# Attention of two query tiles at once, with the values' matrix applied to the result, in a fused FFN–attention–FFN kernel on one core

## The chip, the cores and the metric

The kernel runs on one core of a Trainium2 chip. The metric is the device time of one execution in microseconds, here as the median of the runs shown. Engines are named as in the profile: PE (TensorE's matmuls), PEld (its weight loads), DVE (VectorE), ACT (ScalarE), POOL (GpSimd), SP (SyncE).

## The reference, cut to what matters

The input x is 8 x 1024 x 128 in fp32. Three residual steps follow one another: half of a mixture-of-experts FFN of layernorm(x) (16 experts of 64 units, four chosen per token, and a shared expert), causal attention of layernorm(x), and the same half FFN again. The change is in the attention:

```python
q = einsum('bmd,ed->bme', x, w_q); k = einsum(..., w_k); v = einsum(..., w_v)
scores = einsum('bqd,bkd->bqk', rotate(q), rotate(k)) / sqrt(d)
attn = softmax(where(causal, scores, -inf), axis=-1)
return einsum('bqk,bkd->bqd', attn, v)
```

Here x is the layernorm's output, m = 1024 and d = 128, with one head for each of the 8 sequences.

## The kernel before, in words

A sequence has 8 tiles of 128 tokens. The FFN works on a **group** of four tiles. There are two layers of FFN, 8 sequences and 2 groups each, so 32 groups, and the main loop makes one **pass** for each. A pass first computes the shared expert (L270, then ACT's `ss` at L275 and DVE's product at L276), then eight ups, then nine downs. An up is two matmuls of 512 columns (L283, L284), a Silu on ACT (L286) and a product on DVE (L288) that writes `hidT`. POOL weighs `hidT` by the routing (L292). A down is a matmul of 512 columns (L298); the ninth is followed by a copy of the result on DVE (L306).

Everything else is put by hand into **slots** between these steps: U0 before the first up, U1 to U8 after each up, D0 to D8 after each down. A slot's functions are issued in the order in which they were entered: queries, heads, groups. The order of each engine's instructions is the order of issue. A group's routing for the next pass is spread over the slots: D7 and D8 hold `route_b` (L206), `score` (L211), `top_a` and `top_b`; U1 of the following pass holds `top_c` (ending in `comb`, L243), U3 `spread` (L252), which needs `comb`. U3 also holds `add` of the pass before (L328 on PE, L331 on DVE).

**Attention.** `Heads` belongs to one sequence: it normalizes the tiles, transposes them into `hT`, projects q and k (L367 to L375; two projections, in U3 and U4, of the pass in which the head's first query is and of the pass before) and, in `values`, the values v (L381, L385). A `Query` is one tile of 128 queries, number i from 0 to 7 of its head. It goes through scores (L400 to L407), exp (L411), two `turn`s of up to four transposes each (L427, evacuated by ACT at L431 or by DVE at L433) and `attend` (L439): i + 1 matmuls of 128 columns, then one product-and-sum on DVE (L443) and the two statistics instructions of the next layernorm (L149, L150).

Queries are handed out in order, two or three to a pass. With n = 0, 1, 2 for the first, second and third query of pass p, attend stands in D7 of pass p, U2 of pass p + 1 and U5 of pass p + 1. The queries of passes 3 to 28 are, by number i: (0 1 2) (3 4) (5 6 7) (0 1) (2 3 4) (5 6) (7 0 1) (2 3) (4 5 6) (7 0) (1 2 3) (4 5) (6 7) (0 1) (2 3 4) (5 6) (7 0 1) (2 3) (4 5) (6 7) (0 1 2) (3 4) (5 6 7) (0 1 2) (3 4 5) (6 7). Heads 0 to 7 begin in passes 3, 6, 9, 12, 16, 19, 23 and 26.

**PSUM.** Ups use banks 0 to 3 by turns, so an up needs the bank that DVE's L288 of the up two before has read. The shared expert uses bank 5, projections 4 and 5, scores two banks (2 and 3, or 4 and 5). All smaller work takes banks 6 and 7 in strict turn: `other_bank()` returns the other one at each call. Whoever takes a bank waits for the engine that evacuates what was put there two calls before.

```python
def other_bank():
    spare[0] += 1
    return bank(6 + spare[0] % 2)
```

Of the kernel before, what the change touches and what calls it, by code (L numbers as in the profile page):

```python
# [9 lines left out]
F32 = mybir.dt.float32  # L10
AF = mybir.ActivationFunctionType
ALU = mybir.AluOpType
# [3 lines left out]
P = 128  # L16
# [10 lines left out]
def kernel(  # L27
# [14 lines left out]
    nc = tc.nc  # L42

    B, S, D = x.shape
    E = gate_w.shape[1]
    I = w_sh_down.shape[0]
    NT = S // P
    GT = 4
    NG = NT // GT
    W = GT * P  # L50
# [7 lines left out]
    ln = ctx.enter_context(tc.tile_pool(name="ln", bufs=2))  # L58
    small = ctx.enter_context(tc.tile_pool(name="small", bufs=3))
    work = ctx.enter_context(tc.tile_pool(name="work", bufs=3))  # L60
    big = ctx.enter_context(tc.tile_pool(name="big", bufs=2))
    att = ctx.enter_context(tc.tile_pool(name="att", bufs=2))
# [5 lines left out]
    def bank(i, n=1):  # L68
        return psum[:, i * W : (i + n) * W]
# [3 lines left out]
# [4 lines that stand above are left out]
    def tiles_of(ap):  # L77
        return ap.rearrange("p (j q) -> p j q", q=P)
# [16 lines left out]
    xs, mvs = [None] * B, {}  # L95
# [38 lines left out]
    wqkv = const.tile([P, 3, D], F32, name="wqkv")  # L134
# [8 lines left out]
    def stats(key, b, tiles):  # L143

        if key not in mvs:
            mvs[key] = small.tile([P, NT, 2], F32, tag="mv", name=f"mv_{key}", bufs=16)
        for t in tiles:
            st = small.tile([P, 6], F32, tag="st", name=f"st_{key}_{t}")
            nc.vector.bn_stats(st, xs[b][:, t, :])  # L149
            nc.vector.bn_aggr(mvs[key][:, t, :], st)  # L150

    def deviation(key, g):
        tiles = slice(g * GT, (g + 1) * GT)
        rstd = small.tile([P, GT], F32, tag="rstd", name=f"rs_{key}_{g}")
        nc.vector.tensor_scalar(rstd, mvs[key][:, tiles, 1], LN_EPS, None, ALU.add)
        nc.gpsimd.tensor_tensor(rstd, rstd, neg_half, ALU.pow)  # L156
        return rstd

    def normed(key, b, g, rstd):
        xn = ln.tile([P, GT, D], F32, tag=f"xn{key[0]}", name=f"xn_{key}_{g}")  # L160
        for j in range(GT):
            t = g * GT + j
            nc.vector.tensor_scalar(  # L163
                xn[:, j, :], xs[b][:, t, :], mvs[key][:, t, 0:1], rstd[:, j : j + 1],
                ALU.subtract, ALU.mult,
            )
        return xn

    def transposed(key, g, xn, hT):
        pt = other_bank()  # L170
        for j in range(GT):
            nc.tensor.transpose(tiles_of(pt)[:, j, :], xn[:, j, :], ident)  # L172
        nc.scalar.copy(hT, pt)
# [3 lines left out]
    class Group:  # L177
# [8 lines left out]
        def norm_b(self):  # L186
            self.xn = normed(self.key, self.b, self.g, self.rstd)

        def turn(self):
            self.hT = ln.tile([P, W], F32, tag="hT", name=f"hT_{self.nm}")  # L190
            transposed(self.key, self.g, self.xn, self.hT)
# [147 lines left out]
    class Heads:  # L339
# [5 lines left out]
        def deviations(self):  # L345
            self.rstd = [deviation(self.key, g) for g in range(NG)]
            b = self.b
            self.q = att.tile([P, S], F32, tag="q", name=f"q_{b}")
            self.k = att.tile([P, S], F32, tag="k", name=f"k_{b}")
            self.v = att.tile([P, NT, D], F32, tag="v", name=f"v_{b}")  # L350
            self.rl = small.tile([P, NT], F32, tag="rl", name=f"rl_{b}")
            self.hT = ln.tile([P, S], F32, tag="hTa", name=f"hT_{self.key}", bufs=1)
            self.xn = [None] * NG

        def norm(self, g):
            self.xn[g] = normed(self.key, self.b, g, self.rstd[g])

        def turn(self, g):
            transposed(self.key, g, self.xn[g], self.hT[:, g * W : (g + 1) * W])

        def project(self, w, g):

# [10 lines left out]
            nc.vector.tensor_tensor(r[:, cols], p, cs[:, 0, cols], ALU.mult)  # L373
            nc.gpsimd.tensor_tensor(other, other, cs[:, 1, cols], ALU.mult)
            nc.gpsimd.tensor_tensor(r[:, cols], r[:, cols], other, ALU.add)  # L375

        def values(self, g):
            pv = tiles_of(other_bank())
            for j in range(GT):
                t = g * GT + j  # L380
                nc.tensor.matmul(  # L381
                    pv[:, j, :], self.hT[:, t * P : (t + 1) * P], wqkv[:, 2, :],
                    start=True, stop=True,
                )
            nc.scalar.copy(self.v[:, g * GT : (g + 1) * GT, :], pv)  # L385

    class Query:

# [25 lines left out]
            )  # L414

        def turn(self, half):
            if half == 0:
                self.prT = att.tile([P, NT, P], F32, tag="prT", name=f"prT_{self.nm}")
                rl = self.h.rl[:, self.i : self.i + 1]
                nc.vector.reciprocal(rl, rl)  # L420
            k = half * GT
            n = min(GT, self.i + 1 - k)
            if n <= 0:
                return
            tp = tiles_of(other_bank())
            for j in range(n):
                nc.tensor.transpose(  # L427
                    tp[:, j, :], self.pr[:, (k + j) * P : (k + j + 1) * P], ident
                )
            if half == 0:  # L430
                nc.scalar.copy(self.prT[:, k : k + n, :], tp[:, :n, :])  # L431
            else:
                nc.vector.tensor_copy(self.prT[:, k : k + n, :], tp[:, :n, :])  # L433

        def attend(self):
            i = self.i
            o = other_bank()[:, :D]
            for j in range(i + 1):
                nc.tensor.matmul(  # L439
                    o, self.prT[:, j, :], self.h.v[:, j, :], start=(j == 0), stop=(j == i)  # L440
                )
            xt = xs[self.b][:, i, :]
            nc.vector.scalar_tensor_tensor(  # L443
                xt, o, self.h.rl[:, i : i + 1], xt, ALU.mult, ALU.add
            )
            stats(f"f1_{self.b}", self.b, [i])

# [13 lines left out]
    def at(p, slot, *fs):  # L463
        jobs.setdefault((p, slot), []).extend(fs)
# [3 lines left out]
    def when(p, slot):  # L468
        return p * len(slots) + slots.index(slot)
# [5 lines left out]
    starts, done = {}, {}  # L475
    for p in range(3, 29):
        for n in range(2 if p in (15, 21) or (p % 2 == 0 and p != 26) else 3):
            if not queue:
                continue
            b, i = queue.pop(0)  # L480
            starts.setdefault(b, p)
            q = Query(heads[b], i)
            s, first, e, t0, t1, a = (
                ((p, "U7"), 4, (p, "D0"), (p, "D3"), (p, "D5"), (p, "D7")),
                ((p, "D2"), 2, (p, "D5"), (p, "D8"), (p + 1, "U0"), (p + 1, "U2")),
                ((p, "D4"), 4, (p, "D7"), (p + 1, "U3"), (p + 1, "U4"), (p + 1, "U5")),
            )[n]
            at(*s, lambda q=q, first=first: q.scores(first))
            at(*e, q.exp)
            at(*t0, lambda q=q: q.turn(0))  # L490
            at(*t1, lambda q=q: q.turn(1))
            at(*a, q.attend)
            done[b, i] = when(*a)
    assert not queue


# [1 line left out]
    for b in range(B):  # L498
        h, st = heads[b], starts[b]
        ready = when(turn_of[0, b, 1] + 1, "U7")  # L500
        if b == 0:
            p0, p1 = st - 1, st - 1
            places = ("U8", "D0", "D2", "D3", "D5", "D6", "D7", "D8")
        else:
            p0, p1 = st - 2, st - 1
            places = ("D0", "D3", "D5", "D8", "U1", "U3", "U4", "U6")
        assert ready < when(p0, places[0])
        at(p0, places[0], h.deviations)
        at(p0, places[1], lambda h=h: h.norm(0))
        at(p0, places[2], lambda h=h: h.norm(1))  # L510
        at(p0, places[3], lambda h=h: h.turn(0))
        at(p1, places[4], lambda h=h: h.turn(1))
        at(p1, places[5], lambda h=h: h.project(0, 0))
        at(p1, places[6], lambda h=h: h.project(1, 0))
        at(p1, places[7], lambda h=h: h.values(0))
        at(st, "U3", lambda h=h: h.project(0, 1))
        at(st, "U4", lambda h=h: h.project(1, 1))
        at(st, "U6", lambda h=h: h.values(1))


    for p, gr in enumerate(groups):
# [4 lines left out]
        if p == 1:  # L526
            steps = steps[1:]
            places = [(0, s) for s in ("U3", "U5", "U6", "U8", "D0", "D1", "D2", "D3", "D6")]
        elif p == 2:
            places = [(0, s) for s in ("D0", "D3", "D5", "D6", "D7", "D8", "D8", "D8")]  # L530
            places += [(p - 1, "U1"), (p - 1, "U3")]
        else:
            places = [(p - 2, s) for s in ("U5", "D1", "D4", "D5", "D7", "D7", "D8", "D8")]
# [9 lines left out]
        if gr.layer == 0:  # L543
            t = gr.g * GT
# [5 lines left out]
    for b in range(2, B):  # L550
        p = turn_of[0, b, 0]
# [126 lines left out]
```

## Time and profile before

| what | value |
|---|---|
| median of 3 runs | 1007.22 us (1007.2 to 1007.79) |
| profiled execution | 1008.41 us, span 1006.6 us |
| PE busy | 988.0 us (98%), granted clock 0.998 |
| DVE, ACT, POOL busy | 663.9, 427.4, 451.8 us |
| L439, attend's matmuls | 576 records of 128 columns |
| L381, values' matmuls | 128 records of 128 columns |
| L385, copies of v on ACT | 16, 586 ns each |
| L443 on DVE | 64, 346 ns each |

A matmul of two fp32 operands makes two records, a transpose one. A matmul's record starts when its columns begin to be issued, and its end is modelled; the distance between starts is what it takes of PE. A line of a timeline gives start, duration, engine, source line, operation, tiles written and read, and in brackets how long the engine had been idle and what ended that. A line of waits gives the engine and who waited, for whom, the total in microseconds, how often and the longest.

### The profile page before, as it was taken

The page shows a single profiled execution, that of the slowest core. Times are in us where ns is not written, and L with a number is a line of the kernel's source. Part 1 is how long each engine was busy: PE and PEld are TensorE (multiplying, and loading weights), DVE is VectorE, ACT ScalarE, POOL GpSimd, SP SyncE. Part 2 cuts the span into 40 slices and gives each one's busy share as a digit, 9 for nine tenths or more (in the row PEclk, how much of TensorE's full clock was granted, in tenths as well). Part 3 has the DMA queues.
Part 4 walks back from the last instruction along what each step waited for, and adds up shares of the span by engine and source line. Part 5 has one row for each costly group of instructions (what it writes and reads, how often), then busy time and mean ns, then how long its engine had stood idle before and what let it go on. Part 6 is the DMA issues. An engine that isn't in the chain of part 4 may idle for free.

```text
span 1006.6 us, 11516 instructions
## 1 busy us (share of the span) xinstructions
PE 988.0 (98%) x3590; PEld 516.4 (51%) x3590; DVE 663.9 (66%) x2034; ACT 427.4 (42%) x767; POOL 451.8 (45%) x382
## 2 busy tenths in 40 slices
PE   8999999999999999999999999999999999999998
PEld 5444445554555555545554555545554555455443
DVE  5766877668766667666767656776667757665542
ACT  3334435443544444443544444444444444343321
POOL 2445556244633464234634455234653355322434
PEclk9999999999999999999999999999999999999999
DMA  5645343044303532145403452134422243224440
GB/s 164 167 106 105 86 85 84 3 105 85 85 13 83 117 85 51 35 95 117 86 15 76 90 117 68 29 74 96 95 53 59 60 95 87 47 59 95 96 96 21
DMA packets 56830, 80.23 MB, mean 80 GB/s; under 512 B 3584, under 2 KB 23360, under 8 KB 56640
## 3 DMA queue, kind: packets, MB, share of 16 engines
q1 hardware_dynamic: 55488, 78.23, 34.7%
q10 hardware_dynamic: 1280, 1.26, 0.4%
q8 instruction: 28, 0.46, 0.2%
q14 instruction: 34, 0.28, 0.1%
HBM read 74.24 MB, written 5.24 MB: 79 GB/s over the span
## 4 chain that ended last, share of the span: by engine, by line
PE 89%; DVE 7%; issue 2%; ACT 1%; POOL 0%; ACTq 0%; POOLq 0%; DVEq 0%
PE psum L298 24%; PE psum L283 19%; PE psum L284 19%; PE psum L400 6%; PE psum L439 6%; PE psum L427 3%; PE psum L367 3%; PE psum L270 2%; PE psum L172 2%; DVE hidT L288 2%; PE psum L381 1%; DVE sel L237 1%; PE psum L197 1%; PE psum L328 1%; PE psum L139 1%
## 5 line engine op out<-in xcount | busy, mean ns | idle before, releaser
L292 POOL TENSOR_TENSOR hidT<-hidT,cb 128x512 f32<-128x512 f32 x256 | 323.8, 1271 | 515.7 <-DVE hidT L288 484.1
L284 PE MATMUL psum<-hT,wu 128*128 128x512 f32 x512 | 261.5, 592 | 0.6 <-DVE hidT L288 0.6
L283 PE MATMUL psum<-hT,wg 128*128 128x512 f32 x512 | 261.8, 593 | 0.0
L286 ACT ACTIVATE sg<-psum 128x512 f32<-128x512 f32 x256 | 152.7, 597 | 229.4 <-PE psum L283 216.5
L298 PE MATMUL psum<-hidT,wd 128*128 128x512 f32 x512 | 247.5, 601 | 0.0
L288 DVE TENSOR_TENSOR hidT<-psum,sg 128x512 f32<-128x512 f32 x256 | 175.4, 686 | 96.8 <-PE psum L284 93.8
L284 PEld LDWEIGHTS psum<-hT,wu 128*128 128x128 f32 x512 | 97.2, 190 | 123.4 <-issue 103.0
L298 PEld LDWEIGHTS psum<-hidT,wd 128*128 128x128 f32 x512 | 90.1, 191 | 80.9 <-issue 74.1
L283 PEld LDWEIGHTS psum<-hT,wg 128*128 128x128 f32 x512 | 88.5, 191 | 64.2 <-issue 61.6
L439 PEld LDWEIGHTS psum<-v,prT 128*128 128x128 f32 x576 | 74.4, 192 | 30.6 <-issue 26.3
L431 ACT COPY prT<-psum 128x512 f32<-128x512 f32 (+2 forms) x64 | 32.4, 506 | 108.1 <-PE psum L427 107.4
L439 PE MATMUL psum<-v,prT 128*128 128x128 f32 x576 | 74.6, 275 | 0.0
L400 PE MATMUL psum<-k,q 128*128 128x512 f32 (+2 forms) x192 | 72.4, 486 | 0.0
L443 DVE SCALAR_TENSOR_TENSOR x<-psum,rl,x 128x128 f32<-128x128 f32 x64 | 22.1, 346 | 68.3 <-PE psum L439 38.9
L163 DVE TENSOR_SCALAR xn_f<-x,mv_f,rs_f 128x128 f32<-128x128 f32 x128 | 64.9, 567 | 1.2 <-POOL rs_f L156 1.2
L427 PEld LDWEIGHTS psum<-ident,pr 128*128 128x128 f32 x288 | 36.7, 141 | 50.2 <-issue 34.2
L400 PEld LDWEIGHTS psum<-k,q 128*128 128x128 f32 x192 | 36.5, 190 | 45.9 <-issue 45.2
L406 DVE TENSOR_REDUCE top<-psum 128x1 f32<-128x128 f32 (+3 forms) x64 | 48.5, 758 | 2.2
L427 PE MATMUL psum<-ident,pr 128*128 128x128 f32 x288 | 47.4, 274 | 1.9 <-DVE x L331 1.9
L411 ACT ACTIVATE pr<-psum,top 128x128 f32<-128x128 f32 (+3 forms) x64 | 47.7, 746 | 0.3
L404 DVE TENSOR_TENSOR psum<-psum,causal 128x128 f32<-128x128 f32 x64 | 19.0, 296 | 42.4 <-PE psum L400 42.0
L275 ACT ACT_TABLE_LOAD x31 | 39.8, 1283 | 8.9 <-PE psum L270 8.8
(88 smaller groups left out, 1001.2 us busy)
## 6 DMA issues: line engine op xcount, KB each, us to landing
cb<-cd SPq DMA_DIRECT2D x124, 512.0 KB, 8.3
x<-in_x SPq DMA_DIRECT2D x16, 256.0 KB, 10.3
out_x<-x SPq DMA_DIRECT2D x15, 256.0 KB, 2.4
cb<-cd SPq DMA_DIRECT2D x8, 256.0 KB, 5.2
cd<-cT SPq DMA_DIRECT2D x32, 32.0 KB, 1.8
cs<-in_rope SPq DMA_DIRECT2D x1, 1024.0 KB, 9.8
wg<-in_w_gate ACTq DMA_DIRECT2D x2, 256.0 KB, 6.6
wu<-in_w_up ACTq DMA_DIRECT2D x2, 256.0 KB, 6.0
```

The lines of the kernel that those rows point to most:

```text
L163: nc.vector.tensor_scalar(xn[:, j, :], xs[b][:, t, :], mvs[key][:, t, 0:1], rstd[:, j : j + 1], ALU.subtract, ALU.mult,)
L283: nc.tensor.matmul(g_ps, wg[:, units], self.hT, start=True, stop=True)
L284: nc.tensor.matmul(u_ps, wu[:, units], self.hT, start=True, stop=True)
L286: nc.scalar.activation(sg, g_ps, AF.Silu)
L288: nc.vector.tensor_tensor(hid, u_ps, sg, ALU.mult)
L292: nc.gpsimd.tensor_tensor(hid, hid, self.cb[:, k, :], ALU.mult)
L298: nc.tensor.matmul(self.y, w, h, start=(k == 0), stop=(k == NP))
L400: nc.tensor.matmul(s[:, c:e], h.q[:, i * P : width], h.k[:, c:e], start=True, stop=True)
L406: nc.vector.tensor_reduce(top, s[:, :width], AX.X, ALU.max)
L411: nc.scalar.activation(self.pr[:, : self.width], self.s[:, : self.width], AF.Exp, bias=self.top, scale=SCALE, accum_out=self.h.rl[:, self. ...
L427: nc.tensor.transpose(tp[:, j, :], self.pr[:, (k + j) * P : (k + j + 1) * P], ident)
L439: nc.tensor.matmul(o, self.prT[:, j, :], self.h.v[:, j, :], start=(j == 0), stop=(j == i))
```

## The change

Instead of multiplying probabilities by v, the kernel multiplies them by the layernorm's output and applies the values' matrix to the product: (P xn) Wv instead of P (xn Wv). The projection of v and its copies go, and the head keeps `xn` for its whole life. Queries are taken in pairs, an even one and the odd one behind it. Their transposed probabilities lie side by side, `attend` is called for the odd one alone, with passes of 256 columns (128 for the last key tile, which the even query does not see), and computes the transposed product. ACT copies it to `o`. A new `values` of the query multiplies it by the values' matrix, two matmuls of 128 columns, and does both products-and-sums and both tiles' statistics. `values` stands in U0, U4 or U6 of the pass after, by the place n of the odd query; `attend` stands where that query's attend stood.

```diff
         def turn(self, half):
+            h, q = self.h, self.i % 2
             if half == 0:
-                self.prT = att.tile([P, NT, P], F32, tag="prT", name=f"prT_{self.nm}")
+                if self.i % 2 == 0:
+                    h.prT = att.tile([P, NT, 2, P], F32, tag="prT", name=f"prT_{self.nm}")
+                self.prT = h.prT
...
-                nc.scalar.copy(self.prT[:, k : k + n, :], tp[:, :n, :])
+                nc.scalar.copy(self.prT[:, k : k + n, q, :], tp[:, :n, :])
...
         def attend(self):
+
             i = self.i
-            o = other_bank()[:, :D]
-            for j in range(i + 1):
+            o = other_bank()[:, : 2 * P]
+
+            for j in [0, i] + list(range(1, i)):
+                first = 0 if j < i else P
                 nc.tensor.matmul(
-                    o, self.prT[:, j, :], self.h.v[:, j, :], start=(j == 0), stop=(j == i)
-                )
-            xt = xs[self.b][:, i, :]
-            nc.vector.scalar_tensor_tensor(
-                xt, o, self.h.rl[:, i : i + 1], xt, ALU.mult, ALU.add
-            )
-            stats(f"f1_{self.b}", self.b, [i])
+                    o[:, first:], self.h.xn[:, j, :],
+                    self.prT[:, j, first // P :, :].rearrange("p q t -> p (q t)"),
+                    start=(j == 0), stop=(j == max(i - 1, 1)),
+                )
+            self.o = work.tile([P, 2 * P], F32, tag="o", name=f"o_{self.nm}", bufs=2)
+            nc.scalar.copy(self.o, o)
+
+        def values(self):
+            op = tiles_of(other_bank())
+            for q in range(2):
+                nc.tensor.matmul(
+                    op[:, q, :], self.o[:, q * P : (q + 1) * P], wqkv[:, 2, :],
+                    start=True, stop=True,
+                )
+            for q in range(2):
+                t = self.i - 1 + q
+                xt = xs[self.b][:, t, :]
+                nc.vector.scalar_tensor_tensor(
+                    xt, op[:, q, :], self.h.rl[:, t : t + 1], xt, ALU.mult, ALU.add
+                )
+            stats(f"f1_{self.b}", self.b, [self.i - 1, self.i])
...
-            s, first, e, t0, t1, a = (
-                ((p, "U7"), 4, (p, "D0"), (p, "D3"), (p, "D5"), (p, "D7")),
-                ((p, "D2"), 2, (p, "D5"), (p, "D8"), (p + 1, "U0"), (p + 1, "U2")),
-                ((p, "D4"), 4, (p, "D7"), (p + 1, "U3"), (p + 1, "U4"), (p + 1, "U5")),
+            s, first, e, t0, t1, a, v = (
+                ((p, "U7"), 4, (p, "D0"), (p, "D3"), (p, "D5"), (p, "D7"), (p + 1, "U0")),
+                ((p, "D2"), 2, (p, "D5"), (p, "D8"), (p + 1, "U0"), (p + 1, "U2"), (p + 1, "U4")),
+                ((p, "D4"), 4, (p, "D7"), (p + 1, "U3"), (p + 1, "U4"), (p + 1, "U5"), (p + 1, "U6")),
             )[n]
...
-            at(*a, q.attend)
-            done[b, i] = when(*a)
+            if i % 2:
+                at(*a, q.attend)
+                at(*v, q.values)
+                done[b, i - 1] = done[b, i] = when(*v)
```

The head's `values`, which stood in D8 of pass 2 and U6 of pass 3 for the first head and in U6 of two neighbouring passes for the others, is gone from the lists of places, and `normed` writes into `xn` of the head, a buffer like that of v before.

More of the change, by code (lines that the diff above doesn't have):

```diff
@@ L157, in deviation, with normed @@
         return rstd
-    def normed(key, b, g, rstd):
-        xn = ln.tile([P, GT, D], F32, tag=f"xn{key[0]}", name=f"xn_{key}_{g}")
+    def normed(key, b, g, rstd, xn=None):
+        if xn is None:
+            xn = ln.tile([P, GT, D], F32, tag="xn", name=f"xn_{key}_{g}")
         for j in range(GT):
@@ L349, in deviations @@
             self.k = att.tile([P, S], F32, tag="k", name=f"k_{b}")
-            self.v = att.tile([P, NT, D], F32, tag="v", name=f"v_{b}")
+            self.xn = att.tile([P, NT, D], F32, tag="xna", name=f"xn_{self.key}")
             self.rl = small.tile([P, NT], F32, tag="rl", name=f"rl_{b}")
             self.hT = ln.tile([P, S], F32, tag="hTa", name=f"hT_{self.key}", bufs=1)
-            self.xn = [None] * NG
         def norm(self, g):
-            self.xn[g] = normed(self.key, self.b, g, self.rstd[g])
+            normed(self.key, self.b, g, self.rstd[g], self.xn[:, g * GT : (g + 1) * GT, :])
         def turn(self, g):
-            transposed(self.key, g, self.xn[g], self.hT[:, g * W : (g + 1) * W])
+            transposed(
+                self.key, g, self.xn[:, g * GT : (g + 1) * GT, :], self.hT[:, g * W : (g + 1) * W]
+            )
         def project(self, w, g):
@@ L375, in project @@
             nc.gpsimd.tensor_tensor(r[:, cols], r[:, cols], other, ALU.add)
[L377 to L383, printed above, removed]
-                )
-            nc.scalar.copy(self.v[:, g * GT : (g + 1) * GT, :], pv)
     class Query:
@@ L430, in turn @@
             if half == 0:
-                nc.scalar.copy(self.prT[:, k : k + n, :], tp[:, :n, :])
+                nc.scalar.copy(self.prT[:, k : k + n, q, :], tp[:, :n, :])
             else:
-                nc.vector.tensor_copy(self.prT[:, k : k + n, :], tp[:, :n, :])
+                nc.vector.tensor_copy(self.prT[:, k : k + n, q, :], tp[:, :n, :])
         def attend(self):
             i = self.i
-            o = other_bank()[:, :D]
-            for j in range(i + 1):
+            o = other_bank()[:, : 2 * P]
+            for j in [0, i] + list(range(1, i)):
+                first = 0 if j < i else P
                 nc.tensor.matmul(
-                    o, self.prT[:, j, :], self.h.v[:, j, :], start=(j == 0), stop=(j == i)
-                )
-            xt = xs[self.b][:, i, :]
-            nc.vector.scalar_tensor_tensor(
-                xt, o, self.h.rl[:, i : i + 1], xt, ALU.mult, ALU.add
-            )
-            stats(f"f1_{self.b}", self.b, [i])
+                    o[:, first:], self.h.xn[:, j, :],
+                    self.prT[:, j, first // P :, :].rearrange("p q t -> p (q t)"),
+                    start=(j == 0), stop=(j == max(i - 1, 1)),
+                )
+            self.o = work.tile([P, 2 * P], F32, tag="o", name=f"o_{self.nm}", bufs=2)
[14 more added lines that the diff above has]
+            stats(f"f1_{self.b}", self.b, [self.i - 1, self.i])
     LAG = 4
@@ L502 @@
             p0, p1 = st - 1, st - 1
-            places = ("U8", "D0", "D2", "D3", "D5", "D6", "D7", "D8")
+            places = ("U8", "D0", "D2", "D3", "D5", "D6", "D7")
         else:
             p0, p1 = st - 2, st - 1
-            places = ("D0", "D3", "D5", "D8", "U1", "U3", "U4", "U6")
+            places = ("D0", "D3", "D5", "D8", "U1", "U3", "U4")
         assert ready < when(p0, places[0])
@@ L514 @@
         at(p1, places[6], lambda h=h: h.project(1, 0))
-        at(p1, places[7], lambda h=h: h.values(0))
         at(st, "U3", lambda h=h: h.project(0, 1))
         at(st, "U4", lambda h=h: h.project(1, 1))
-        at(st, "U6", lambda h=h: h.values(1))
     for p, gr in enumerate(groups):
```

## The prediction

> **What bounds the kernel now.** I read the page first, then the waits of PE alone, the chain of waits, and the timeline at the seams between two passes.
>
> ```profile
> PE 988.0 (98%) x3590; PEld 516.4 (51%) x3590; DVE 663.9 (66%) x2034; ACT 427.4 (42%) x767; POOL 451.8 (45%) x382
> ...
> PE 89%; DVE 7%; issue 2%; ACT 1%; POOL 0%; ACTq 0%; POOLq 0%; DVEq 0%
> ```
>
> PE sets the end; the clock row is at 9 throughout. Two things can move the time: what PE has to issue, and where PE waits.
>
> ```profile
> PE psum L328 <- DVE x L443: 3.9, 6, 1.0
> PE psum L252 <- DVE comb L243: 2.7, 3, 2.3
> PE psum L427 <- DVE x L331: 1.9, 5, 0.4
> PE psum L252 <- DVE x L443: 1.7, 3, 0.8
> ...
> PE psum L284 <- DVE hidT L288: 0.6, 1, 0.6
> ```
>
> Those are PE's waits in the body, nearly all on DVE, and the timeline puts them in U2 to U4, just after a seam. They are counted from a modelled end; from start to start each is 0.16 longer (0.77 shown at seam 13 is 0.93). I call a seam by the pass that begins there, and count from the start of its first L270.
>
> Seam 13, after pass 12 with queries 7 and 0, from the timeline:
>
> ```profile
> 419.02 1.02 PE L270 MATMUL psum<-hT,ws 128*128 128x512 f32 x2
> ...
> 422.15 0.69 DVE L276 TENSOR_TENSOR shared<-psum,ss 64x512 f32<-64x512 f32 x1
> ...
> 422.88 0.69 DVE L288 TENSOR_TENSOR hidT<-psum,sg 128x512 f32<-128x512 f32 x1
> ...
> 424.40 1.02 PE L284 MATMUL psum<-hT,wu 128*128 128x512 f32 x2
> ...
> 425.49 0.27 DVE L243 SCALAR_TENSOR_TENSOR comb<-sel,tot 128x64 f32<-128x64 f32 x1
> ...
> 426.24 0.34 DVE L443 SCALAR_TENSOR_TENSOR x<-psum,rl,x 128x128 f32<-128x128 f32 x1
> ...
> 426.63 0.30 PE L252 MATMUL psum<-ident,comb 128*64 128x128 f32 x1 [0.77 <-DVE x L443]
> ```
>
> DVE works without a gap from L276 on. The first hidT is done at 4.55, and the third up's L284, which needs that bank, comes at 5.38: 0.8 to spare. comb is done at 6.74. PE waits at L252 for the bank that L443 frees.
>
> Seam 11, after queries 2 and 3:
>
> ```profile
> 357.56 0.60 PE L328 MATMUL psum<-ident,yT 128*128 128x128 f32 x4
> ...
> 358.96 1.02 PE L284 MATMUL psum<-hT,wu 128*128 128x512 f32 x2
> 359.02 0.69 DVE L373 TENSOR_TENSOR q<-psum,cs 128x512 f32<-128x512 f32 x1 [1.08 <-ACT o_q L372]
> ...
> 359.63 0.68 DVE L331 SCALAR_TENSOR_TENSOR x<-psum,x 128x512 f32<-128x512 f32 x1
> ```
>
> Where a projection stands in U3, L373 waits on ACT with L331 queued behind it, so the add's bank is free at 360.31, while U3's PE work ends at 359.82. Nothing asks for that bank now at this seam; five others with a turn in U4 pay 0.54 each (L427 <- L331).
>
> **Columns on PE.** The chain gives the pace of both widths:
>
> ```profile
> 416.32 1.78 PE psum L439 x16
> ...
> 433.80 0.43 PE psum L400 x2
> ```
>
> A 128-wide record is 0.1113; a 256-wide one 0.2158 (mean start to start of the 32 at L400). Per head the change issues sixteen 256-wide and four 128-wide matmuls for 36 of 128: the same columns. 128 times (4 x 0.1113 - 2 x 0.2158) = 1.7 us gained, all on the path. The values' matmuls are 64 x 2 records before and after, 14.3 us, only moved.
>
> The Trainium skill (TensorE: Matmul & The Clock Gate, Back-to-back issue gap) puts sustained matmuls at about 81 ns for 128 columns and 131 for 512, far from proportional. An estimate along that line (98 ns for 256, a record taken as one matmul) is 16 us saved, 991 in all; the rows here say otherwise.
>
> **ACT and copies.** Sixteen v copies of 0.586 go, 32 o copies of 128x256 come; the prT copy of that shape takes 0.372 (bounds 0.266 and 0.586, its 128 and 512 forms). ACT is 42% busy and between attend and values PE has at least one up (1.72) or, at U0, a down and L270 (0.86 each): nothing, and 0.2 to 0.5 a pair if that cover failed. prT is written with gaps of 128; no row shows that, the contiguous rows are nearest: nothing, at most 0.1 a copy, off the path. The weights o and xn are loaded like v (0.19, hidden).
> One consequence: the o copy at D7 stands before a third query's exp on ACT, and L270 needs bank 5, which that exp reads if the query is over 3. Copy plus 0.91 or 1.12 of exp end after L270's turn: 0.36 at seams 6 and 26, 0.15 at 28 (in their totals below).
>
> **DVE: the pair's burst.** Two L443 (0.346) and two stats now stand together, 1.55 (two steps of 0.37 and two of 0.40 between starts; one L443 with its stats takes 0.90 to the end). Where a pass's first query is odd (seams 5, 6, 9, 10, 13, 14, 19, 20, 25, 26, 28), the burst lands in U0, between L276 and the first hidT, and everything after moves with it: hidT, then comb, then L331. The even query beside it no longer attends in U2, which takes up to 1.56 of PE work out of the cover, while values add 0.445.
> Seam 13: hidT is free at 4.54 - 0.10 (no L443 in D7) + 1.55 + 0.05 = 6.04; PE arrives at 5.38 - 0.22 + 0.445 = 5.60: stall 0.44. PE would then be at L252 at 6.89 + 0.44 = 7.33; comb frees it at 6.64 + 1.60 = 8.24: 0.91 more. 1.35 against 0.93 now: +0.42.
> The 0.05 is the release that seam 3 shows (hidT ends at 5.90, L284 starts at 5.95).
> The others alike, from their own rows (hidT and comb ends now, L284's and L252's starts now, less the even query's matmuls, plus values): Seams 5 and 25: hidT 6.36 against PE 6.15, 0.21; L252 0.06 behind comb; no wait now: +0.27 each. Seams 9 and 19: 6.63 against 5.94, 0.69, and 0.06: +0.75 each. Seams 10 and 20: 6.04 against 5.60, 0.44; comb at 8.24 against 7.62, 0.62; they lose 1.16 now: -0.1 each. Seam 14: 0.44, and 8.24 against 7.82, 0.42; now 0.38: +0.48. Seams 6 and 26: hidT 0.22 later still, as ACT's ss comes behind the exp: 6.61 against 5.94, 0.67, and 0.36 at L270: +1.0 each; the 0.54 of L427 stays. Seam 28: 6.36 against 5.71, 0.65; comb 0.46; L270 0.15; a turn in U4 behind L331 0.2; now 0.40: +1.06.
>
> With seam 13 the sum is **+5.8**. Its bounds are -4.0, if all is covered and today's waits go, and 11 times the whole burst less 4.0 that they wait now, 13.
>
> The Trainium skill (PSUM — Partial Sum Buffer, Engine vs sequencer instructions) takes VectorE's queue as strict first in, first out, which speaks against this change: hidT cannot pass the burst. The rows above agree (L331 sits behind a waiting L373); were it untrue, the 5.8 would go.
>
> **Even-first seams.** The burst moves to U4, where DVE has caught up. The L443 of U2 is gone and ACT frees that bank. Of the waits now, 7 and 17 lose 0.61 each, 21 0.16. 4, 24 and 27 lose 0.72, but the spread then waits for ACT's prT copy (seam 28 shows 0.40 for 512 columns, so 0.30 for 384): 0.42 each. Sum **-2.6**. What is late next: values in U4 takes the bank of the add in U3, so where a projection stands there it meets the 0.54 of seam 11. At 8, 12 and 18 this replaces the wait of L427; at 11, 15, 16, 22 and 23 it is new: **+2.7**.
>
> **Moved work.** values(0) of head 0 stood in D8 before seam 3, where PE already waits 0.80 for hidT and DVE is bound by the projection in D7. Without its 0.89 the same wait is 0.89 longer: **+0.9**. The other heads' values leave U6, where no wait follows. Query matmuls in D7 grow or vanish, and no wait stands there: L206's input is ready 1.4 before it even without them. POOL has 3.5 or more to spare before each down.
>
> **Sum.** -1.7 + 5.8 - 2.6 + 2.7 + 0.9 = +5.1. The profiled span of 1006.6 becomes 1011.7; that execution took 1008.4 (1.8 around the span), the median is 1007.2, so 1012.3.
>
> **Rivals.**
> A, faster: DVE has more slack at the seams than one trace shows, and the burst is covered. Then the odd-first seams lose their present waits too (1.16, 0.93, 0.38, 1.16, 0.40, together 4.0): -1.7 - 2.6 - 4.0 + 3.6 = -4.7, 1002.5. It decides if hidT may come 1.55 later; the rows give 0.8.
> B, no change: the burst costs half because the stats overlap and the bank of U4 is free in time: -1.7 + 2.9 - 2.6 + 0.9 = -0.5, 1006.7. For it: single stats overlap by 0.1. Against: L331's lag is tied to PE's projection.
> C, slower still: values wait for the o copy because ACT is behind an exp, 0.2 to 0.5 for 11 to 32 pairs, some +5: 1017.3. Against it: ACT idles before most of its rows.
> That the change would not do what it says shows in no row: equal columns leave it little to do on PE.
>
> **How the numbers follow.** Forecast 0.62, A 0.12, B 0.14, C 0.12. About 0.2% (2 us) is what a measurement can tell from no change. Slower 0.62 + 0.12 = 0.74, same 0.14, faster 0.12. The range leaves out A and the far half of C, and has half a microsecond around B and C for the copies: 1006.0 to 1016.5.
>
> **What would show it.** Right: PE waits at L284 on hidT at some ten seams, at the values' line on L331 at eight, none of L328 on L443; PE's busy time down by little; the seam 13 wait at L252 on comb. Wrong: no hidT wait in U2, or values waiting on the o copy.

## The result, and the profile after

The changed kernel takes 1012.6 us (median of 6 runs, 1011.65 to 1013.52) against 1007.39 us (6 runs): 1.0052 times, 95% interval 1.0042 to 1.0062. It is slower by 5.2 us; the prediction said 1012.3. The profiled execution took 1013.49 us with a span of 1011.7.

The page of the kernel after, its busy times and its chain by engine:

```profile
PE 989.9 (98%) x3334; PEld 505.9 (50%) x3334; DVE 660.0 (65%) x2034; ACT 429.0 (42%) x783; POOL 450.1 (44%) x382
...
PE 87%; DVE 9%; ACT 2%; issue 1%; POOL 0%; ACTq 0%; DVEq 0%; POOLq 0%
```

PE has 256 records fewer and is busy for 1.9 us more, 989.9 against 988.0; DVE's share of the chain rises from 7 to 9%. No engine has much more work to do (ACT, with 16 instructions more, 1.6 us). The waits of PE alone show what it is instead. Lines have moved: up's matmuls are L284 and L285, the product that writes `hidT` L289, add L329 and L332, `comb` L244, spread L253, a turn L423, attend L438, the copy of `o` L444, values L449 and their sums L456.

```profile
PE psum L253 <- DVE comb L244: 4.4, 6, 2.3
PE psum L449 <- DVE x L332: 3.0, 8, 0.4
PE psum L173 <- DVE x L456: 2.2, 2, 1.1
PE psum L285 <- DVE hidT L289: 1.9, 5, 0.9
...
PE psum L423 <- DVE x L332: 0.8, 2, 0.4
```

The six waits of L328 on L443 and the three of L252 on it are gone. In their place stand eight of values on the add's L332, hidT and comb more often, and two of a head's turn (L173) on the sums of values, which the prediction did not have. The longest wait of the first row, 2.3, is one in pass 0 that the kernel before has too; the prediction's row of `comb` contains it, and it is no wait of the body, but its sum does not use it.

Seam 13 in the timeline of the kernel after:

```profile
419.28 1.02 PE L271 MATMUL psum<-hT,ws 128*128 128x512 f32 x2
...
422.40 0.69 DVE L277 TENSOR_TENSOR shared<-psum,ss 64x512 f32<-64x512 f32 x1
423.13 0.61 DVE L456 SCALAR_TENSOR_TENSOR x<-psum,rl,x 128x128 f32<-128x128 f32 x2
...
424.47 0.67 DVE L289 TENSOR_TENSOR hidT<-psum,sg 128x512 f32<-128x512 f32 x1
...
425.20 1.12 PE L285 MATMUL psum<-hT,wu 128*128 128x512 f32 x2 [0.15 <-DVE hidT L289]
...
427.07 0.27 DVE L244 SCALAR_TENSOR_TENSOR comb<-sel,tot 128x64 f32<-128x64 f32 x1
...
427.40 0.30 PE L253 MATMUL psum<-ident,comb 128*64 128x128 f32 x1 [0.64 <-DVE comb L244]
```

Two sums and two tiles' statistics occupy DVE from 423.13 to 424.47, between `shared` and the first hidT. The third up waits for hidT (0.32 from start to start), and L253 for comb (0.80): 1.12 where it was 0.93. In front of it PE has 0.22 of query work less and 0.445 of values more.

And values in U4 at seam 11:

```profile
358.20 0.60 PE L329 MATMUL psum<-ident,yT 128*128 128x128 f32 x4
...
359.66 0.69 DVE L376 TENSOR_TENSOR q<-psum,cs 128x512 f32<-128x512 f32 x1 [1.36 <-ACT o_q L375]
...
360.26 0.68 DVE L332 SCALAR_TENSOR_TENSOR x<-psum,x 128x512 f32<-128x512 f32 x1
...
361.00 0.71 PE L449 MATMUL psum<-wqkv,o 128*128 128x128 f32 x4 [0.38 <-DVE x L332]
```

The bank that nothing asked for before is now asked for too early, and PE loses 0.54 from start to start.

### The profile page after: what moved, and what is told of

Read it like the earlier page. It is cut to its first block, busy times and chain, and to the rows that moved or that the text cites. A ratio compares the mean times of both kernels' runs of the same rounds, so it can differ in the third digit from the quotient of the medians.

```text
span 1011.7 us, 11037 instructions
## 1 busy us (share of the span) xinstructions
PE 989.9 (98%) x3334; PEld 505.9 (50%) x3334; DVE 660.0 (65%) x2034; ACT 429.0 (42%) x783; POOL 450.1 (44%) x382
## 4 chain that ended last, share of the span: by engine, by line
PE 87%; DVE 9%; ACT 2%; issue 1%; POOL 0%; ACTq 0%; DVEq 0%; POOLq 0%
PE psum L299 24%; PE psum L285 18%; PE psum L284 18%; PE psum L438 6%; PE psum L393 6%; PE psum L423 3%; PE psum L370 2%; PE psum L271 2%; PE psum L173 2%; PE psum L449 1%; DVE hidT L289 1%; PE psum L198 1%; DVE sel L238 1%; DVE shared L277 1%; PE psum L139 1%
## 5 line engine op out<-in xcount | busy, mean ns | idle before, releaser
L285 PE MATMUL psum<-hT,wu 128*128 128x512 f32 x512 | 262.3, 594 | 2.5 <-DVE hidT L289 1.9
L284 PE MATMUL psum<-hT,wg 128*128 128x512 f32 x512 | 261.7, 593 | 0.0
L299 PE MATMUL psum<-hidT,wd 128*128 128x512 f32 x512 | 247.7, 601 | 0.0
L289 DVE TENSOR_TENSOR hidT<-psum,sg 128x512 f32<-128x512 f32 x256 | 174.3, 687 | 99.9 <-PE psum L285 95.6
L285 PEld LDWEIGHTS psum<-hT,wu 128*128 128x128 f32 x512 | 96.6, 190 | 127.7 <-issue 98.0
L299 PEld LDWEIGHTS psum<-hidT,wd 128*128 128x128 f32 x512 | 90.2, 191 | 80.9 <-issue 74.4
L284 PEld LDWEIGHTS psum<-hT,wg 128*128 128x128 f32 x512 | 90.7, 191 | 71.2 <-issue 68.2
L307 DVE COPY yT<-psum 128x512 f32<-128x512 f32 x31 | 21.4, 691 | 108.4 <-PE psum L299 108.4
L164 DVE TENSOR_SCALAR xn_f<-x,mv_f,rs_f 128x128 f32<-128x128 f32 x128 | 68.9, 598 | 1.9 <-POOL rs_f L156 1.9
L438 PE MATMUL psum<-prT,xn_a 128*128 128x256 f32 (+1 forms) x320 | 67.6, 358 | 0.0
L438 PEld LDWEIGHTS psum<-prT,xn_a 128*128 128x128 f32 x320 | 57.0, 190 | 20.7 <-issue 12.4
L423 PEld LDWEIGHTS psum<-ident,pr 128*128 128x128 f32 x288 | 36.7, 141 | 43.8 <-issue 36.9
L423 PE MATMUL psum<-ident,pr 128*128 128x128 f32 x288 | 47.2, 273 | 0.8 <-DVE x L332 0.8
L444 ACT COPY o<-psum 128x256 f32<-128x256 f32 x32 | 11.9, 372 | 83.9 <-PE psum L438 83.9
```

Of the source, the lines that this page charges most:

```text
L164: nc.vector.tensor_scalar(xn[:, j, :], xs[b][:, t, :], mvs[key][:, t, 0:1], rstd[:, j : j + 1], ALU.subtract, ALU.mult,)
L284: nc.tensor.matmul(g_ps, wg[:, units], self.hT, start=True, stop=True)
L285: nc.tensor.matmul(u_ps, wu[:, units], self.hT, start=True, stop=True)
L289: nc.vector.tensor_tensor(hid, u_ps, sg, ALU.mult)
L299: nc.tensor.matmul(self.y, w, h, start=(k == 0), stop=(k == NP))
L423: nc.tensor.transpose(tp[:, j, :], self.pr[:, (k + j) * P : (k + j + 1) * P], ident)
```

## The experiments

The theory is the prediction's: the new product costs PE nothing, and the time lies in where its follow-up work stands. The rival is that the two-step product itself (attend, copy, values) costs, wherever it stands. Where a timing is compared with a trace, I take the stretch from the first L271 (L270) of pass 2 to the end, called the body. Each body is that of one profiled execution. The first two passes, with the loads, take 63.0 to 65.1 us in these traces whichever the kernel; why they vary was not tried.

Ratios are against runs of the kernel before on the same chip, with medians of 1006.98 to 1007.39.

| kernel | median us | ratio to before, 95% | body us |
|---|---|---|---|
| before | 1006.98 to 1007.39 | | 941.7 |
| after | 1012.6 | 1.0052 (1.0042 to 1.0062) | 946.7 |
| e1, values later (first) | 1005.57 | 0.9987 (0.9978 to 0.9996) | 939.9 |
| e2, values later (second) | 1009.16 | 1.0023 (1.0014 to 1.0033) | 943.6 |
| e3, both | 1002.47 | 0.9955 (0.9941 to 0.9969) | 936.8 |
| e4, 128 columns | 1013.96 | 1.0073 (1.0060 to 1.0085) | 948.7 |
| e5, statistics apart | 1008.24 | 1.0013 (1.0004 to 1.0023) | 942.7 |
| e6, e3 and exp earlier | 1001.10 | 0.9946 (0.9933 to 0.9959) | 935.7 |
| e7, e3 and projection earlier | 1001.35 | 0.9949 (0.9936 to 0.9962) | 935.8 |
| e8, all | 1000.16 | 0.9937 (0.9923 to 0.9951) | 934.6 |
| e9, before, projection earlier | 1006.61 | 0.9992 (0.9983 to 1.0001) | 940.8 |
| e10, after, turn later | 1009.40 | 1.0018 (1.0009 to 1.0027) | 944.1 |

**e1: the burst out of U0.**

```diff
-                ((p, "U7"), 4, (p, "D0"), (p, "D3"), (p, "D5"), (p, "D7"), (p + 1, "U0")),
+                ((p, "U7"), 4, (p, "D0"), (p, "D3"), (p, "D5"), (p, "D7"), (p + 1, "U5" if p < 27 else "U4")),
```

> Values of a pair whose odd query is the first of its pass stand in U5 instead of U0 (U4 for the last such pass). Theory (DVE's burst in U0 delays hidT and comb, and the bank of values is held): the waits at the eleven odd-first seams, 9.6 us in the trace of the changed kernel, shrink to about 3.3 (comb at 13, ACT's prT copy at 10, 14, 20 and 28, the exp and L331 at 6 and 26), and the 0.1 behind each wait goes with them: 7.5 less than the changed kernel, about 1005. Rival (the time lies in the two-step product itself, attend, copy, values, wherever it stands): within 1 us of 1012.6.

Measured 1005.57; the body is 6.8 shorter than that of the changed kernel. The waits at the eleven seams fall from 9.6 to 3.5. The rival is refuted: with the same instructions, some of them in another slot, the time is 7.0 us below the changed kernel and just under the kernel before. Waits of PE in e1:

```profile
PE psum L449 <- DVE x L332: 3.0, 8, 0.4
PE psum L253 <- DVE comb L244: 2.9, 4, 2.3
...
PE psum L285 <- DVE hidT L289: 0.9, 1, 0.9
```

hidT holds PE once (at seam 3), and L173 no longer waits for L456. The eight waits of values on L332 are as they were: they belong to the other move.

**e2: values out of U4.**

```diff
-                ((p, "D2"), 2, (p, "D5"), (p, "D8"), (p + 1, "U0"), (p + 1, "U2"), (p + 1, "U4")),
+                ((p, "D2"), 2, (p, "D5"), (p, "D8"), (p + 1, "U0"), (p + 1, "U2"), (p + 1, "U5" if p < 28 else "U4")),
```

> Values of a pair whose odd query is the second of its pass stand in U5 instead of U4 (U4 for the last pass). Theory (values in U4 takes the bank of the add and waits 0.54 for L331 behind the projection): the wait goes at seams 11, 15, 16, 22 and 23 and comes back as a wait of the turn L423 at 8, 12 and 18, so 2.7 and five times 0.1 less: about 1009.4. Rival (two-step product itself): no change, 1012.6. Second rival (a full DVE queue in U4, not the bank): the wait moves to U5 with the burst, no change either, but waits stand at the ups behind U5.

Measured 1009.16, body 3.1 shorter. The waits of PE in e2 show that five are gone and three have gone back to the turn:

```profile
PE psum L423 <- DVE x L332: 1.9, 5, 0.4
```

There is no row of L449 on L332 left. The five are three new ones (seams 8, 12, 18) and the two that the changed kernel had (6, 26). It is the bank: the burst follows to U5, and no up behind it waits.

**e3: both.**

> Both moves at once. Theory: they touch different seams and add, 7.5 + 3.2 less, about 1002, below the kernel before (1007.4). Rival (two-step product itself): 1012.6. If the bursts only collide elsewhere, between 1005 and 1009.

Measured 1002.47: 0.9955 of the kernel before. The body is 9.9 shorter than the changed kernel's, the sum of 6.8 and 3.1.

Seam 13 in the timeline of e3:

```profile
417.73 0.70 DVE L277 TENSOR_TENSOR shared<-psum,ss 64x512 f32<-64x512 f32 x1
...
418.45 0.69 DVE L289 TENSOR_TENSOR hidT<-psum,sg 128x512 f32<-128x512 f32 x1
...
421.40 0.30 PE L253 MATMUL psum<-ident,comb 128*64 128x128 f32 x1 [0.19 <-DVE comb L244]
```

hidT follows `shared` at once, and 0.36 from start to start is left of 1.12.

**e4: the columns by themselves.**

```diff
-            for j in [0, i] + list(range(1, i)):
-                first = 0 if j < i else P
+            for q in range(2):
+                for j in range(i + q):
...
-                    o[:, first:], self.h.xn[:, j, :],
+                    o[:, q * P : (q + 1) * P], self.h.xn[:, j, :], self.prT[:, j, q, :],
```

> The changed kernel with attend in passes of 128 columns, one query's key tiles after the other's, so 288 matmuls again instead of 160. Theory (a record costs its columns and 3 to 4 ns more): 1.7 us more than the changed kernel, 1014.3. Rival (narrow passes are held by their weight loads, as the page's 81 ns against 131 would have it): 10 us more or over.

Measured 1013.96, body 2.0 longer. The longest attend in the chain of waits, of the kernel after and then of e4:

```profile
415.12 3.25 PE psum L438 x16
```

```profile
415.85 3.35 PE psum L438 x30
```

The same 3,840 columns, in 16 records of 0.203 (fourteen wide, two narrow) or in 30 of 0.112. From start to start all of L438 takes 62.4 us in the kernel after and 64.2 in e4. The 256-wide passes are worth 1.8 us here and no more; over 256 records that is 7 ns a record, not the 3 to 4 of the expectation. The medians differ by 1.4, and the intervals of the two ratios touch, so the size rests on the rows. An estimate from the sustained figures of the Trainium skill (TensorE: Matmul & The Clock Gate, Back-to-back issue gap), 81 ns for 128 columns and 131 for 512, gives the narrow form some 16 us more. For these fp32 matmuls the rows decide against it.

**e5: the length of the burst.** The statistics of a pair whose values stand in U0 go to U5; the sums stay.

```diff
-            stats(f"f1_{self.b}", self.b, [self.i - 1, self.i])
+        def statistics(self):
+            stats(f"f1_{self.b}", self.b, [self.i - 1, self.i])
...
+                w = (p + 1, "U5" if p < 27 else "U4") if n == 0 else v
+                at(*w, q.statistics)
```

> The changed kernel, but where values stand in U0 only the two products-and-sums stay there; the pair's statistics go to U5 (U4 for the last such pass). This takes 0.80 of the burst's 1.34 out of DVE's queue before hidT and comb, and leaves the values' matmuls, their bank and when it comes free as they were. Theory (the burst's length in DVE's queue): hidT's waits at 9, 10, 13, 14, 19, 20 go, comb's at 10, 13 and 20 halve, the bank waits stay (1.28 at seams 5 and 25, 0.87 at 6 and 26): 3.7 less than the changed kernel, 1008.9. Rival (it is the bank that values hold, or the copy of o, and not the length): 1012.6, with the same waits.

Measured 1008.24, body 4.0 shorter. Seam 13 in the timeline of e5:

```profile
420.82 0.61 DVE L456 SCALAR_TENSOR_TENSOR x<-psum,rl,x 128x128 f32<-128x128 f32 x2
...
421.35 0.68 DVE L289 TENSOR_TENSOR hidT<-psum,sg 128x512 f32<-128x512 f32 x1
...
424.28 0.30 PE L253 MATMUL psum<-ident,comb 128*64 128x128 f32 x1 [0.25 <-DVE comb L244]
```

With L271 at 416.97 the seam waits 0.41 instead of 1.12, while L456 and its bank stand where they stood. The bank waits stay to the digit: 1.28 at seams 5 and 25. So the burst costs in two separate ways at the eleven seams, by its length in DVE's queue and, at two of them, by the bank of values. The Trainium skill (PSUM — Partial Sum Buffer, Engine vs sequencer instructions) says that VectorE's queue is strict first in, first out. This agrees: with 0.8 us taken out ahead of it, hidT starts 4.38 after L271 instead of 5.19.

**e10: the bank at seams 5 and 25.**

```diff
-            places = ("D0", "D3", "D5", "D8", "U1", "U3", "U4")
+            places = ("D0", "D3", "D5", "D8", "U2", "U3", "U4")
```

> The changed kernel with the heads' second turn in U2 instead of U1 (heads 1 to 7). Theory (at seams 5 and 25 the turn waits 1.28 for the bank that the values of U0 hold until DVE reaches their two sums): a turn one up later finds the bank free and hidT ready, 2.6 less and 0.2 behind the waits, 1009.8. Rival (DVE is that late anyhow, and any PE work in its place waits): the wait goes to L285 on hidT, 1012.0 or more.

Measured 1009.40, body 2.6 shorter. One up later the turn starts without a wait, and the up behind it too, as the timeline of e10 at seam 5 shows:

```profile
157.21 0.60 PE L173 MATMUL psum<-ident,xn_a 128*128 128x128 f32 x4
157.65 1.02 PE L284 MATMUL psum<-hT,wg 128*128 128x512 f32 x2
158.51 1.02 PE L285 MATMUL psum<-hT,wu 128*128 128x512 f32 x2
```

**e6, e7, e8: what e3 leaves.** e6 moves the third query's exp ahead of the copy of `o` (`(p, "D4"), 4, (p, "D6")`), e7 head 0's projections a slot earlier (`"D7", "D5", "D6"` as the last three places), e8 both.

> Both moves of values, and the third query's exp in D6 instead of D7, ahead of the o copy on ACT. Theory (L271 waits for bank 5 because the exp is queued behind the copy of o): the 0.33 at seams 6 and 26 and the 0.11 at 28 go with 0.1 each behind them, 1.0 less than with both moves alone, 1001.5. Rival (the exp itself is late, not its place): no change, 1002.5.

> Both moves of values, and head 0's two projections of its first half one slot earlier (D5, D6), its second turn in D7. Theory (at seam 3 DVE is bound by the last projection, and the values that stood between it and the seam are gone): the waits of 1.58 at seam 3 fall to some 0.3 to 0.5, 1.3 less, 1001.2. Rival (seam 3 waits for the routing's comb and scores, whatever the projection): no change, 1002.5.

> Both moves of values, the earlier exp and the earlier projections of head 0. If each takes away a wait of its own they add: 1000.2, 0.7 per cent under the kernel before. If seam 3 only hands its wait on, 1001.5.

Measured 1001.10, 1001.35 and 1000.16. The bodies are 1.1, 1.0 and 2.2 shorter than e3's, so each takes away a wait of its own. In e6 L271 starts on time at all three seams. In e7 the waits at seam 3 are 0.54 instead of 1.58. e8 is the best version: 0.9937 of the kernel before. The page of e8:

```profile
PE 984.9 (99%) x3334; PEld 506.4 (51%) x3334; DVE 657.5 (66%) x2034; ACT 429.0 (43%) x783; POOL 450.4 (45%) x382
```

**e9: what of that is the places' own.** The kernel before with the same earlier projections.

> The kernel before the change, with head 0's two projections of its first half in D5 and D6 and its second turn in D7 (values stay in D8). How much of the gain of the best version is the places' alone: the wait of 0.80 at seam 3 and 0.1 behind it go, 0.9 less than before, 1006.2. If it were 5 us or more, the best version would owe little to the change.

Measured 1006.61, ratio 0.9992, interval up to 1.0001; the body is 0.9 shorter and seam 3 has no wait. So of the 6.8 us by which the median of e8 beats the kernel before, about one comes from this move alone. The exp's move has nothing to mend there, since no copy of `o` stands before it.

One rival was not tried: the kernel before with its other work in better slots. At seams 4 to 28 it has 10.3 us of waits from start to start, and 7.0 of them are nine waits for L443, the sum behind attend; e8 has 5.2 left. So the runs show that e8 beats the kernel as it was. They do not show how much of that the two-step product itself is worth, beyond the 1.8 of its wider passes.

## Why the prediction was right, point by point

The total is right to 0.3 us, and that closeness is luck; the terms are not all so good. Waits are counted from start to start at their seams.

**Columns**, -1.7: measured 64.2 to 62.4, -1.8, and e4 gives it back. Right.

**Odd-first seams**, +5.8: their waits went from 5.1 to 9.6, +4.5. The mechanism is shown by e1 and e5; several sizes were off, in both directions. The burst lasts 1.34, not 1.55: two sums one behind the other take 0.53 where 0.74 was taken (0.37 had been read between a sum and the statistics of its own tile), and the statistics 0.40 a tile, as taken. The 0.10 taken off for the missing L443 of D7 did not come: at seam 13 `shared` starts 3.12 after L271, and 3.13 before. And PE never waits for hidT at seams 6, 26 and 28, where 0.65 or 0.67 was expected. The timeline of the kernel after, seam 6:

```profile
188.85 1.13 PE L271 MATMUL psum<-hT,ws 128*128 128x512 f32 x2 [0.17 <-ACT pr L404]
...
191.32 0.69 DVE L277 TENSOR_TENSOR shared<-psum,ss 64x512 f32<-64x512 f32 x1
...
193.83 0.68 DVE L289 TENSOR_TENSOR hidT<-psum,sg 128x512 f32<-128x512 f32 x1
...
194.88 1.02 PE L285 MATMUL psum<-hT,wu 128*128 128x512 f32 x2
```

The wait at L271 (0.33 at 6 and 26, 0.11 at 28) holds PE while DVE goes on, and `ss` was not late at all: `shared` starts 2.47 after L271, where 2.80 stood before. That wait was counted as a loss on top of hidT's, but it paid for a part of hidT's. Seams 9 and 19 came out at 0.34 each for 0.75, seams 10 and 20 at 1.34 and 0.99 for 1.06.

**The step that failed** is in the same term: seams 5 and 25, forecast at 0.27, cost 1.28 each. In the pass before a head begins, its second turn stands in U1 and takes the bank that values took in U0. The working counted banks for the slots U3 and U4 and not for U1. The turn at seam 5 in the timeline of the kernel before, without a wait, and in that of the kernel after:

```profile
155.94 0.60 PE L172 MATMUL psum<-ident,xn_a 128*128 128x128 f32 x4
```

```profile
156.27 0.61 DVE L456 SCALAR_TENSOR_TENSOR x<-psum,rl,x 128x128 f32<-128x128 f32 x2
...
156.93 0.66 PE L173 MATMUL psum<-ident,xn_a 128*128 128x128 f32 x4 [1.12 <-DVE x L456]
```

e10 takes these two waits away and gains 2.6.

**Even-first seams**, -2.6 and +2.7: measured 5.14 to 5.19, together +0.05. Seam by seam it is as forecast: nothing at 7, 17 and 21, 0.30 on ACT's prT copy at 4, 24 and 27, 0.54 at 8, 11, 12, 15, 16, 18, 22 and 23. The 0.54 is the same at every seam where this wait stands, before the change, after it and in e2, whatever DVE did earlier; this is why the term came out so well. e2 shows the mechanism.

**Head 0's values**, +0.9: 0.80 to 1.58 at seam 3, +0.8. Work that leaves PE in front of a DVE-bound wait gains nothing; e7 shows that the projection binds it.

**What was left out of the sum.** After a wait, the second record of the matmul comes 0.10 late as well: the third up at seam 13 takes 1.12 instead of 1.02, L449 at seam 11 0.71 instead of 0.61. The body has 19 such pairs after the change and 1 before, +1.9. The terms as measured are -1.8 + 4.5 + 0.05 + 0.8 + 1.9 = +5.4; the body grew by 5.0, and the rest is spread over gaps of under 0.06. So the total was hit by luck: an odd-first sum that was 1.3 too large made up for most of a term of 1.9 that was missing.

**A sign that did not come.** PE's busy time was to fall by a little and rose by 1.9. The profile counts the 0.10 of each second record as busy, and 0.16 of each wait, and there are 14 waits more at the seams: by estimate 1.9 + 2.2 - 1.8 = +2.3.

**The rivals.** A (the burst is covered) fails in the trace: hidT's wait stands in U2. B (half a burst, the bank of U4 free in time) fails at the eight rows of L449. C (values wait for the copy of `o`) has no row among PE's waits: at seam 11 the copy starts at 355.82 and takes 0.37, so that it ends nearly five microseconds before values start.

## What to carry to other kernels

When a product is rewritten at equal column count, look for its price in what follows it: which queue its evacuation enters, what is queued behind it, and who takes its bank next. Where one engine sets the end and another is 65% busy, a step of 1.3 us can cost nothing or all of its length, depending on the slot; moving two slots here turned 0.5% slower into 0.45% faster. Count every user of a bank that is taken in turn, from the slot of the change to the second call behind it, and not only at the slots where waits are seen today.

## What was not expected of the hardware

A wait of PE costs more than the wait. After each wait of a two-record matmul in the body, its second record began 0.10 us later than in an undisturbed row, at L285 (512 columns), at L449 (128) and at L271. The timeline of the kernel after shows it at seam 3, where both weight loads begin only when the wait ends:

```profile
95.00 0.30 PEld L285 LDWEIGHTS psum<-hT,wu 128*128 128x128 f32 x2 [1.20 <-DVE yT L307]
95.00 1.13 PE L285 MATMUL psum<-hT,wu 128*128 128x512 f32 x2 [0.37 <-DVE yT L307]
```

Undisturbed, a load of 0.19 lies beside the matmul before. The same 0.10 stands 29 times in the kernel after, and as often in the kernel before, at an L299 behind the routing's L198, where PE waits for no other engine. The last records of L198 are 7 ns apart, too short for a load to lie beside them. One of these places, in the kernel after:

```profile
119.01 0.30 PEld L299 LDWEIGHTS psum<-hidT,wd 128*128 128x128 f32 x2 [0.20 <-issue]
119.01 1.98 PE L299 MATMUL psum<-hidT,wd 128*128 128x512 f32 x4
```

So the 0.10 goes with a load that could not start early, and not only with a wait for another engine. That the load is the reason was not tried. For a turn of four transposes the price is smaller: 0.66 after the wait at seam 5, where undisturbed turns take 0.60.
